# VectorE writes masks into PSUM ahead of the score matmuls, in an attention block followed by six local-attention layers

## The chip, the core and the metric

The kernel runs on one core of a Trainium2 chip. The metric is the device time of one execution in microseconds. Before the change it is 2072.76 us, the median of 3 runs (2070.76 to 2073.34).

The core has five engines that run their own instruction streams in order: TensorE (PE in the profile, with its weight loads listed apart as PEld), VectorE (DVE), ScalarE (ACT), GpSimd (POOL) and SyncE (SP), which here only issues DMAs. PE writes its results into PSUM; the other tiles lie in SBUF.

## The reference, cut to what matters

The input x has 4 sequences of 512 tokens with 128 features. The first stage is a pre-norm causal attention with 16 heads of 64. The future isn't masked out: -50 is added to its scores. The second stage is a pre-norm stack of 6 layers, each a local attention and a GEGLU feed-forward network, with residuals around them.

```python
x = x + attn(layernorm(x), Wq, Wk, Wv, Wr)
    # scores = q k^T / 8 + (-50) * triu(ones, 1); softmax; times v; @ Wr
x = x + ffn(layernorm(x), ...)
    # for each of 6 layers:
    #   t = attn_layer(shift_tokens(x)) + x
    #   x = ffn_layer(shift_tokens(t)) + t
def local_attention(q, k, v):          # windows of 32 tokens
    bk2, bv2 = (look(bk), look(bv))    # a window and the one before it
    mask = (it < jb) | (it > jb + w) | (jb == -1)
    sim = einsum('bhwie,bhwje->bhwij', bq, bk2) * QK_SCALE
    sim = where(mask, -finfo.max, sim)
    out = einsum('bhwij,bhwje->bhwie', softmax(sim, -1), bv2)
```

In a layer q and k are scaled to unit norm per head, multiplied by learned scales and rotated by position. The feed-forward part is a layer norm, a product with W1, a gate by GELU and a product with W2.

## The kernel before

Everything on the engines is issued in an order written out by hand. All matmuls have fp32 operands, but for the two masks, which are bf16.

**First stage** (lines 296 to 495). The work is cut into `Rows`: one sequence b, one pair of heads c (of 8) and one block t of 128 query rows (of 4). The loop runs over 64 slots m; slot m works on two `Rows`, t = 0 and 1 in an even slot, t = 2 and 3 in an odd one. Within a slot:

- `times_v1` (L384) multiplies probabilities of a pair of heads some slots back by v into `o1`, half of the products in each of two slots. After the second half VectorE copies the result to SBUF (L403) at once.
- `scores` (L302) takes a buffer `sc` of two PSUM banks, one per head, and issues four matmuls: for each half of the 512 keys, one for each of the two heads. The two heads' operands lie in different halves of the partitions. There are two `sc` buffers, so a row block takes the buffer of the block two before it, which must have been read by its exponentials.
- `penalty` (L317) adds -50 above the diagonal with two more matmuls per block: identity times a 128x128 triangle `pen`, accumulated into the diagonal block's columns. Both blocks' scores are issued first, then both penalties.
- VectorE takes the negated maximum over the keys (`maximum`, L335); ScalarE takes the exponentials (L348), in two parts with a bias lower by 50 for the keys beyond the diagonal block, and their sums; VectorE adds and inverts the sums (`inverse`, L358 and L359); GpSimd multiplies (`normalise`, L362).
- The probabilities of the slot before are transposed on PE (L373) and copied back by ScalarE (L377) and VectorE (L381). A projection of q, k or v for later slots (L271, L277, L287) lies between.

**The layers** (lines 498 to 1102). A `Unit` is one layer i, one sequence b, one block T of 128 tokens: 96 units in order. `slot(n, ...)` works on four of them at once: it finishes the output of unit n-1, does the attention of unit n, transposes q and k of unit n+1, and projects unit n+2 (`new`). A feed-forward network of a sequence is spread over later slots by three tables: its token shift (`move`), its norm (`norm`: mean, variance and scale in three slots), and its GEGLU steps (`geglu`: three chunks of hidden columns and the output product in four slots). From n = 7 to n = 94 every slot has a GEGLU step, at its end.

The order in `slot` that matters here: `scores(u)` on PE, the projection of Q for `new` with ScalarE's squares, the exponentials, norm steps, the output projection of unit n-1, the rotation of Q (two VectorE products, L570 and L576, and a sum on GpSimd, L587), the transposes of the probabilities (L661, copied by ScalarE, L664) with the projection of K between them, `times_v` (L737, with VectorE's reciprocal and product L746 and L747), the rotation of K, `transpose_o` (L753, VectorE), the sums of squares of Q and of K (`sum_squares`, L565, VectorE), the transposes of q and k, the projection of V, the guard of the norms (L590), the GEGLU step, and the inverse norms (L598 to L606).

`scores` (L684) starts with eight matmuls of a 32x32 identity with a band mask of 64 columns, repeated for 8 pairs of heads (L690). They start the accumulation of every place in two PSUM banks. The 64 products of q and k follow (L700). Then VectorE takes the maximum (L710) and subtracts it (L712), and ScalarE takes the exponential (L718).

PSUM for the layers is three tiles of two banks that rotate (`two_t`, by `part[0] = -n % 3`) and two single banks. In slot n tile 1 of the rotation takes Q's projection, tile 2 K's, tile 0 V's. Tile 2 of slot n is tile 0 of slot n+1, the one that `scores` uses.

Weights: `do_project` loads part j of the next layer's Wqkv right after the last unit of a layer has been projected with it (`load_part`, L501, 512 KB each, on SP's queue). SP also issues the two shifted copies of v in each slot (`shift_v`, L650), the output weights and the feed-forward weights, in program order; a DMA that must wait for an engine holds up those behind it.

## Time and profile before

| | |
|---|---|
| runs, median (lowest to highest) | 2072.76 us (2070.76 to 2073.34) |
| the profiled execution | 2072.4 us, span 2070.6 us |
| PE busy, by matmuls | 2028.4 us (98%), 34382 records |
| VectorE busy | 1640.8 us (79%) |
| ScalarE busy | 1368.2 us (66%) |
| GpSimd busy | 1316.5 us (64%) |

An fp32 matmul shows as two records on PE and two weight loads. The ends of matmuls are modelled, so the distance between starts says more than a duration. By stage, from the trace's busy times in windows: from 52 to 530 us (first stage) PE is busy 475.25 us, VectorE 329.27, ScalarE 308.69, GpSimd 246.42; from 680 to 1990 us (layers) PE 1301.86, VectorE 1114.82, ScalarE 918.19, GpSimd 920.37.

These are groups of the page: line, engine, operation, output and inputs with their shapes, count, then busy time and mean duration, then the engine's idle time before them and what ended most of it.

```profile
L335 DVE TENSOR_REDUCE nm<-ps_sc 128x2 f32<-128x1024 f32 x128 | 155.9, 1218 | 62.9 <-PE ps_sc L323 62.8
L746 DVE RECIPROCAL rden<-ps_att 128x8 f32<-128x8 f32 x192 | 38.8, 202 | 176.8 <-PE ps_att L737 176.7
L565 DVE TENSOR_REDUCE ss<-sq 128x16 f32<-128x1024 f32 x192 | 221.1, 1190 | 0.0
```

The first line is the maximum in the first stage: 128 of them, 1218 ns each, and VectorE idled 62.9 us before them, nearly all of it until the penalty matmuls were done. The second is the reciprocal in the layers, before which VectorE idles 176.8 us in total for `times_v`. The third is the sums of squares, before which it never idles.

### The profile page before, as it was taken

The numbers are of one execution on the slowest core, as the hardware profiler recorded it, in microseconds if no ns is written. First come the engines' busy times: TensorE is split into PE (matmuls) and PEld (weight loads), VectorE is DVE, ScalarE is ACT, GpSimd is POOL, SyncE is SP. The second block draws the span as 40 slices with busy tenths as digits, with TensorE's granted clock in tenths as the row PEclk, the third lists the DMA queues.
The fourth block names the chain that finished last, engine by engine and source line by source line (L and its number), as shares of the span: only waits on it lengthen the run. The fifth ranks groups of instructions, "written<-read, shape, count | busy, mean of one in ns | idle before, by whom it ended". The sixth has DMA issues, their size and how long they took to land.

```text
span 2070.6 us, 77263 instructions
## 1 busy us (share of the span) xinstructions
PE 2028.4 (98%) x34382; PEld 1329.1 (64%) x34382; DVE 1640.8 (79%) x2240; ACT 1368.2 (66%) x2678; POOL 1316.5 (64%) x1432
## 2 busy tenths in 40 slices
PE   7999999999999999999999999999999999999998
PEld 5665555655466666666666666666666666666665
DVE  3766766767698888888888888888888888888885
ACT  3665665666455766676776676776667776677763
POOL 1554554555677677667767667667677767667762
PEclk8999999999999999999999999999999999999999
DMA  3000000000011121111211112111121111211110
GB/s 127 1 1 1 1 1 1 1 1 1 12 44 36 42 67 44 44 44 33 77 44 34 54 36 64 53 35 44 46 64 44 38 51 46 67 41 44 38 45 27
DMA packets 34968, 77.44 MB, mean 37 GB/s; under 512 B 4686, under 2 KB 18764, under 8 KB 34636
## 3 DMA queue, kind: packets, MB, share of 16 engines
q1 hardware_dynamic: 33932, 70.79, 11.8%
q8 instruction: 272, 4.46, 0.9%
q10 hardware_dynamic: 704, 1.70, 0.2%
q14 instruction: 60, 0.49, 0.1%
HBM read 23.50 MB, written 1.05 MB: 12 GB/s over the span
## 4 chain that ended last, share of the span: by engine, by line
PE 91%; DVE 5%; ACT 2%; POOL 1%; issue 1%; DMA 0%; SPq 0%; POOLq 0%; ACTq 0%
PE ps_proj L548 23%; PE ps_one L661 12%; PE ps_one L762 7%; PE ps_att L737 7%; PE ps_sc L308 6%; PE ps_o L393 6%; PE ps_att L700 5%; PE ps_pt L373 5%; PE ps_proj L812 3%; PE ps_proj L813 3%; PE ps_proj L832 3%; PE ps_pj L287 1%; PE ps_att L690 1%; PE ps_pj L277 1%; PE ps_pj L271 1%; PE ps_pj L407 1%
## 5 line engine op out<-in xcount | busy, mean ns | idle before, releaser
L587 POOL TENSOR_TENSOR rot<-rot,t 128x1024 f32<-128x1024 f32 x192 | 454.2, 2366 | 232.6 <-DVE t L576 220.1
L548 PE MATMUL ps_proj<-wqkv,xs 128*128 128x512 f32 x1152 | 569.0, 602 | 0.5 <-PE ps_one L661 0.2
L362 POOL TENSOR_TENSOR pr<-pr,den 128x1024 f32<-128x1024 f32 x128 | 241.0, 1893 | 248.3 <-DVE den L359 238.5
L606 POOL TENSOR_TENSOR rot<-rot,ss 128x1024 f32<-128x1024 f32 x192 | 361.3, 1903 | 7.4
L560 ACT ACTIVATE sq<-ps_proj 128x1024 f32<-128x1024 f32 x192 | 196.4, 1023 | 93.8 <-PE ps_proj L548 93.6
L548 PEld LDWEIGHTS ps_proj<-wqkv,xs 128*128 128x128 f32 x1152 | 188.2, 190 | 102.0 <-issue 92.1
L570 DVE TENSOR_TENSOR rot<-ps_proj,lt 128x1024 f32<-128x1024 f32 x192 | 233.3, 1215 | 10.2 <-ACT sq L560 10.0
L576 DVE TENSOR_TENSOR t<-ps_proj,lt 128x1024 f32<-128x1024 f32 x192 | 232.9, 1213 | 0.0
L348 ACT ACTIVATE pr<-ps_sc,nm 128x128 f32<-128x128 f32 (+3 forms) x448 | 220.3, 509 | 11.8 <-DVE nm L335 8.6
L565 DVE TENSOR_REDUCE ss<-sq 128x16 f32<-128x1024 f32 x192 | 221.1, 1190 | 0.0
L661 PEld LDWEIGHTS ps_one<-ident,rot 128*128 128x128 f32 x1536 | 172.7, 141 | 61.2 <-issue 51.2
L661 PE MATMUL ps_one<-ident,rot 128*128 128x128 f32 x1536 | 205.1, 276 | 1.1 <-POOL xs L170 0.6
L335 DVE TENSOR_REDUCE nm<-ps_sc 128x2 f32<-128x1024 f32 x128 | 155.9, 1218 | 62.9 <-PE ps_sc L323 62.8
L664 ACT COPY pT<-ps_one 128x512 f32<-128x512 f32 x192 | 110.0, 587 | 136.6 <-PE ps_one L661 136.6
L762 PEld LDWEIGHTS ps_one<-aT,wo 128*128 128x128 f32 x1536 | 182.9, 192 | 23.6 <-issue 17.7
L762 PE MATMUL ps_one<-aT,wo 128*128 128x128 f32 x1536 | 189.1, 276 | 0.3 <-ACT tmp_t L852 0.2
L746 DVE RECIPROCAL rden<-ps_att 128x8 f32<-128x8 f32 x192 | 38.8, 202 | 176.8 <-PE ps_att L737 176.7
L648 ACT COPY vt<-ps_proj 128x512 f32<-128x512 f32 x192 | 103.1, 590 | 96.4 <-PE ps_proj L548 96.4
L373 PEld LDWEIGHTS ps_pt<-ident,pr 128*128 128x128 f32 x1024 | 117.4, 142 | 58.5 <-issue 47.4
L664 ACT COPY qT<-ps_one 128x512 f32<-128x512 f32 x192 | 103.1, 589 | 66.1 <-PE ps_one L661 66.1
L377 ACT COPY pT<-ps_pt 128x512 f32<-128x512 f32 x128 | 75.6, 591 | 98.0 <-PE ps_pt L373 98.0
L373 PE MATMUL ps_pt<-ident,pr 128*128 128x128 f32 x1024 | 135.9, 274 | 3.0 <-DVE pT L381 2.4
(178 smaller groups left out, 3763.2 us busy)
## 6 DMA issues: line engine op xcount, KB each, us to landing
vs<-vt SPq DMA_DIRECT2D x96, 390.0 KB, 3.7
vs<-vt SPq DMA_DIRECT2D x72, 130.0 KB, 3.6
wqkv<-in_wqkv_dram SPq DMA_DIRECT2D x18, 512.0 KB, 4.0
vs<-in_zeros_dram SPq DMA_DIRECT2D x24, 130.0 KB, 3.7
wo<-in_wo_dram SPq DMA_DIRECT2D x6, 512.0 KB, 4.2
w<-in_w_dram SPq DMA_DIRECT2D x6, 341.0 KB, 5.9
xr<-in_x_dram SPq DMA_DIRECT2D x3, 256.0 KB, 7.6
scales<-in_scales_dram SPq DMA_DIRECT2D x6, 128.0 KB, 3.1
```

The lines of the kernel that those rows point to most:

```text
L348: nc.scalar.activation(self.pr[:, h, cols], self.sc[:, h, cols], AF.Exp, bias=self.nm[:, part_, h : h + 1], accum_out=self.den[:, part_, h ...
L362: nc.gpsimd.tensor_tensor(self.pr, self.pr, self.den[:, 0].unsqueeze(2).to_broadcast([P, 2, S]), ALU.mult)
L373: nc.tensor.transpose(pt[:, k * P : (k + 1) * P], self.pr[:, h, k * P : (k + 1) * P], ident)
L548: mm(p[:, c, :], lhsT=u.xs[:, u.T * P : (u.T + 1) * P], rhs=wpart[j][:, c * 512 : (c + 1) * 512], start=True, stop=True,)
L565: nc.vector.tensor_reduce(u.ss[:, j * HEADS : (j + 1) * HEADS], heads(u.sq[j]), AX.X, ALU.add)
L570: nc.vector.tensor_tensor(heads(t0), heads(pf), lt[:, u.T, 2 * j].unsqueeze(1).to_broadcast([P, HEADS, HD]), ALU.mult)
L576: nc.vector.tensor_tensor(t1.rearrange("p (h t d) -> p h t d", t=2, d=half), pf.rearrange("p (h t d) -> p h t d", t=2, d=half)[:, :, ::-1, :],
L587: nc.gpsimd.tensor_tensor(u.r[j], u.r[j], u.t1, ALU.add)
L606: nc.gpsimd.tensor_tensor(heads(u.r[j]), heads(u.r[j]), u.ss[:, j * HEADS : (j + 1) * HEADS].unsqueeze(2).to_broadcast([P, HEADS, HD]), AL ...
L661: nc.tensor.transpose(tp[:, c * P : (c + 1) * P], src[:, (4 * g + c) * P : (4 * g + c + 1) * P], ident)
L664: nc.scalar.copy(dst[:, 4 * g : 4 * g + 4, col0 : col0 + P], tp.rearrange("p (c t) -> p c t", c=4))
L762: mm(y[:, 0:P], lhsT=wo_w[0][:, k, :], rhs=u.aT[:, g].rearrange("p (j f) -> p j f", f=P)[:, :, f0 : f0 + W], start=(k == 0), stop=(k == NC ...
```

## The change

- First stage: from slot 4 on the penalty matmuls go. In the slot before, VectorE copies the triangle, now also in fp32 (`pen32`, 64 KB, loaded on SP's queue behind `pen`), into the diagonal block's columns of both heads in the next `sc` buffer (`preset`), ahead of `inverse`, for either row block. The score matmuls add to it.
- `scores` goes over the keys in three pieces instead of two, in every slot: the diagonal block (128 columns), the other half of the keys (256), and the neighbour of the diagonal block (128). So it issues six matmuls per block instead of four.
- The copy of `o1` to SBUF is issued behind the first block's maximum instead of ahead of it.
- Layers: in a slot with a GEGLU step VectorE copies the mask of the next unit, now an fp32 constant (`mask`, 128 KB, loaded on SP's queue ahead of the tables), into tile 2 of the rotation, 1024 columns, after the rotation of K. The next slot's `scores` then issues no band matmuls.
- In slots with n >= 0 the sum of squares of Q moves from behind `transpose_o` to ahead of `times_v`.
- The load of Q's part of the next layer's Wqkv moves from behind Q's projection on SP's queue to behind the transposes of the probabilities on ScalarE's queue.

```diff
+            def preset(self):
+                sc = self.sc = ps1.tile([P, 2, S], F32, tag="sc", name="ps_sc", bufs=2)
+                nc.vector.tensor_copy(
+                    sc[:, :, self.t * P : (self.t + 1) * P], pen32.unsqueeze(1).to_broadcast([P, 2, P])
+                )
             def scores(self):
...
-                for k0 in range(0, S, S // 2):
+                sc, far = self.sc, (1 - t // 2) * 2
+                for k, (k0, n) in enumerate(((t, 1), (far, 2), (t ^ 1, 1))):
+                    cols = slice(k0 * P, (k0 + n) * P)
                     for h in range(2):
                         rows = slice(h * HD, (h + 1) * HD)
                         mm(
-                            sc[:, h, k0 : k0 + S // 2],
+                            sc[:, h, cols],
                             lhsT=qs[b, c][rows, t * P : (t + 1) * P],
-                            rhs=ks[b, c][rows, k0 : k0 + S // 2],
-                            start=(k0 == 0),
-                            stop=False,
+                            rhs=ks[b, c][rows, cols],
+                            start=(k == own),
+                            stop=own or k == 2,
...
             for r in now:
-                r.penalty()
+                if r.late:
+                    r.penalty()
...
             if now:
                 now[0].maximum()
+            if m >= 4:
+                keep()
...
             if now:
+                if 3 <= m < last - 1:
+                    rows[2 * m + 2].preset()
                 now[0].inverse()
                 now[0].normalise()
...
+                if 3 <= m < last - 1:
+                    rows[2 * m + 3].preset()
                 now[1].inverse()
...
+    def preset(u):
+        u.sc = two_t(2, "ps_att")
+        nc.vector.tensor_copy(
+            u.sc.rearrange("p a (c n) -> p a c n", n=2 * W),
+            mask[:, min(u.T, 1)].unsqueeze(2).to_broadcast([P, 2, NC, 2 * W]),
+        )
     def scores(u):
-        sc = two_t(0, "ps_att")
-        for j, h, x_, p0 in PLACES:
+        sc = two_t(0, "ps_att") if u.sc is None else u.sc
+        for j, h, x_, p0 in PLACES if u.sc is None else ():
...
+    def next_part(u, j):
+        if u.b + 1 == B and u.T + 1 == NT and u.i + 1 < L:
+            wpart[j] = load_part(u.i + 1, j, nc.sync if j else nc.scalar)
...
             transpose_p(u, 1)
+        if new:
+            next_part(new, 0)
...
+        if new and n >= 0:
+            sum_squares(new, 0)
         if u:
             times_v(u, 0)
             times_v(u, 1)
...
         if new:
             rotate(new, 1)
             add_rotated(new, 1)
+        if new and geglu and n >= 0:
+            preset(nxt)
         if u:
             transpose_o(u)
+        if new and n < 0:
+            sum_squares(new, 0)
         if new:
-            sum_squares(new, 0)
             sum_squares(new, 1)
```

More of the change, by code (lines that the diff above doesn't have):

```diff
@@ L61, in body @@
     band = const.tile([P, 2, 2 * W], BF16, tag="band", name="band")
+    mask = const.tile([P, 2, 2, 2 * W], F32, tag="mask", name="mask")
     ident16 = const.tile([P, P], BF16, tag="ident16", name="ident16")
@@ L195, in body @@
         pen = s1.tile([P, P], BF16, tag="pen", name="pen")
+        pen32 = s1.tile([P, P], F32, tag="pen32", name="pen32")
         xr = [s1.tile([P, NT, EMB], F32, tag="xr", name=f"xr{b}", bufs=2) for b in range(B)]
@@ L205, in body @@
                 nc.sync.dma_start(out=pen, in_=a["pen"])
+                nc.sync.dma_start(out=pen32, in_=a["pen32"])
         for t_, n_ in ((wq, "wq"), (wk, "wk"), (wv, "wv")):
@@ L210, in body @@
         nc.sync.dma_start(out=band, in_=a["band"])
+        nc.sync.dma_start(out=mask, in_=a["mask"])
         nc.sync.dma_start(out=tabs, in_=a["tabs"])
@@ L299, in __init__ @@
             def __init__(self, b, c, t):
-                self.b, self.c, self.t = b, c, t
+                self.b, self.c, self.t, self.sc = b, c, t, None
+            def preset(self):
[3 more added lines that the diff above has]
+                )
             def scores(self):
                 b, c, t = self.b, self.c, self.t
-                sc = self.sc = ps1.tile([P, 2, S], F32, tag="sc", name="ps_sc", bufs=2)
-                for k0 in range(0, S, S // 2):
+                own = self.sc is not None
+                self.late = not own
+                if not own:
+                    self.sc = ps1.tile([P, 2, S], F32, tag="sc", name="ps_sc", bufs=2)
+                sc, far = self.sc, (1 - t // 2) * 2
+                for k, (k0, n) in enumerate(((t, 1), (far, 2), (t ^ 1, 1))):
+                    cols = slice(k0 * P, (k0 + n) * P)
                     for h in range(2):
@@ L402, in times_v1 @@
                 at = aTs[b, c] = s1c.tile([P, S], F32, tag="aT1", name="aT1", bufs=NC + 2)
-                nc.vector.tensor_copy(at, o)
+                return lambda: nc.vector.tensor_copy(at, o)
+            return lambda: None
         def project_out1(b, y):
@@ L427, in body @@
                 g = m // 2 - 2
-                times_v1(g // NC, g % NC, odd)
+                keep = times_v1(g // NC, g % NC, odd)
             for r in now:
@@ L499, in body, with load_part @@
     s2a = ps2a = s2b = s2 = ps_one = kT_first = vts = None
-    def load_part(i, j):
+    def load_part(i, j, eng=nc.sync):
         w = wts.tile([P, INNER], F32, tag=f"wqkv{j}", name=f"wqkv{j}_{i}")
-        nc.sync.dma_start(out=w, in_=a["wqkv"][i, :, j * INNER : (j + 1) * INNER])
+        eng.dma_start(out=w, in_=a["wqkv"][i, :, j * INNER : (j + 1) * INNER])
         return w
@@ L541, in __init__ @@
             self.i, self.b, self.T = i, b, T
-            self.r, self.sq = [None, None], [None, None]
+            self.r, self.sq, self.sc = [None, None], [None, None], None
     def project(u, j, c0=0, c1=2):
@@ L884, in do_project @@
         project(u, j, c0, c1)
-        if c1 == 2 and u.b + 1 == B and u.T + 1 == NT and u.i + 1 < L:
-            wpart[j] = load_part(u.i + 1, j)
+        if j and c1 == 2:
+            next_part(u, j)
+    def next_part(u, j):
+        if u.b + 1 == B and u.T + 1 == NT and u.i + 1 < L:
+            wpart[j] = load_part(u.i + 1, j, nc.sync if j else nc.scalar)
     def first_slot():
@@ L899, in first_slot @@
         square(new, 0)
-        times_v1(B - 1, NC - 2, 1)
+        times_v1(B - 1, NC - 2, 1)()
         rotate(new, 0)
@@ L911, in first_slot @@
         inverse_norms(new)
-        times_v1(B - 1, NC - 1, 1)
+        times_v1(B - 1, NC - 1, 1)()
         second_step()
@@ L1141, in _constants @@
         band[r : r + W, 1] = np.where(seen, 0.0, NEG)
+    mask = np.repeat(band[:, 1:2, None, :], 2, 2).repeat(2, 1)
+    for r in range(0, P, HD):
+        mask[r + W : r + HD] = mask[r : r + W]
+        mask[r : r + W, 0, 0] = band[r : r + W, 0]
     band = band.astype(ml_dtypes.bfloat16)
@@ L1146, in _constants @@
     zeros = np.zeros((W, 2, NC, HD + 1), f)
-    return {"tabs": tabs, "band": band, "pen": pen, "ident16": ident16, "zeros": zeros}
+    return {"tabs": tabs, "band": band, "mask": mask, "pen": pen, "pen32": pen.astype(f), "ident16": ident16, "zeros": zeros}
 def kernel(**inputs):
```

## The prediction, made before the changed kernel was run

> **What bounds the kernel now.** I read the page first: the busy line and the chain that ended last.

> ```profile
> span 2070.6 us, 77263 instructions
> ...
> PE 91%; DVE 5%; ACT 2%; POOL 1%; issue 1%; DMA 0%; SPq 0%; POOLq 0%; ACTq 0%
> ```

> TensorE's matmuls are 91% of that chain, so an instruction taken from PE counts fully unless another engine is late soon after. The second view is the timeline of two slots of the first stage (start, duration, engine, line, operation, count, in brackets the idle time before and what ended it).

> ```profile
> 421.41 2.00 PE L308 MATMUL ps_sc<-k,q 64*128 64x256 f32 x16
> 423.34 0.40 PE L323 MATMUL ps_sc<-pen,ident 128*128 128x128 bf16 x4
> 423.57 1.04 PE L373 MATMUL ps_pt<-ident,pr 128*128 128x128 f32 x8
> 423.66 1.23 DVE L335 TENSOR_REDUCE nm<-ps_sc 128x2 f32<-128x1024 f32 x1 [2.17 <-PE ps_sc L323]
> ...
> 428.19 2.00 PE L308 MATMUL ps_sc<-k,q 64*128 64x256 f32 x16
> 428.29 0.48 ACT L348 ACTIVATE pr<-ps_sc,nm 128x256 f32<-128x256 f32 x1
> 428.96 0.49 DVE L358 TENSOR_TENSOR den<-den 128x2 f32<-128x2 f32 x1 [1.00 <-ACT pr L348]
> ```

> PE starts one thing as the last stream ends: scores take 1.93 us (421.41 to 423.34), the penalty 0.23 (423.34 to 423.57). VectorE waits 2.17 us for both rows' scores and the penalty. The third view is the timeline of the layers, per engine: PE, VectorE, PE's weight loads, ScalarE.

> ```profile
> 1176.80 1.02 PE L813 MATMUL ps_proj<-hT,w 128*128 128x512 f32 x2
> 1177.75 0.41 PE L690 MATMUL ps_att<-band,ident 64*32 64x512 bf16 x8
> 1177.98 1.46 PE L700 MATMUL ps_att<-kT_first,qT 64*32 64x64 f32 x128
> ...
> 1183.83 1.04 PE L661 MATMUL ps_one<-ident,pr 128*128 128x128 f32 x8
> ```

> ```profile
> 1171.87 0.21 DVE L746 RECIPROCAL rden<-ps_att 128x8 f32<-128x8 f32 x1 [2.02 <-PE ps_att L737]
> ...
> 1174.69 1.22 DVE L576 TENSOR_TENSOR t<-ps_proj,lt 128x1024 f32<-128x1024 f32 x1
> 1175.82 1.23 DVE L753 STREAM_TRANSPOSE aT<-on 128x1024 f32<-128x1024 f32 x1
> 1176.98 2.30 DVE L565 TENSOR_REDUCE ss<-sq 128x16 f32<-128x1024 f32 x2
> 1179.35 0.75 DVE L820 SCALAR_TENSOR_TENSOR tmp_t<-ps_proj,vecs,tmp_t 128x512 f32<-128x512 f32 x1
> ```

> ```profile
> 1183.64 1.00 PEld L661 LDWEIGHTS ps_one<-ident,pr 128*128 128x128 f32 x8 [0.47 <-ACT pr L718]
> ```

> ```profile
> 1182.52 1.06 ACT L718 ACTIVATE pr<-pr 128x1024 f32<-128x1024 f32 x1
> ```

> The band's matmuls hold PE for 0.23 us (1177.75 to 1177.98; eight run side by side). VectorE is nearly full but stands idle about 2 us before L746 in each slot. The weight load of the probabilities' transpose is released by the exponential only 0.19 us before its matmul starts: little is to be gained there beyond that.

> **The change part by part.** *Penalty, first stage.* Slots 4 to 63 lose four penalty matmuls: 60 x 0.23 = 13.8 us off PE.

> *Scores in three pieces.* All 64 slots now issue 12 matmuls in place of 8, with the same columns. The nearest row for a 128-column record is L373: 8 in 0.88 us (423.57 to the next start, 424.45), 0.110 each, against 0.43 / 4 = 0.1075 for a quarter of a 512-column record (L813, 0.86 for two). Eight records more at 0.0025 is 0.02; I take 0.03 a slot, +1.9 us. Bounds: nothing, and a 128-column pair of heads as dear as a 256-column one (1.93 / 4 = 0.48, two pairs more, +0.97 a slot, +62 us). I stay at the low end because loads aren't the limit in the trace: L700 loads 128 weights of 32 columns in about 1.4 us of its slot, 0.011 us each, so 24 loads of 128 columns would need 24 x 4 x 0.011 = 1.1 us, under 1.93.

> [...]

> *Presets, first stage.* Two VectorE copies of 128x256 from SBUF into PSUM a slot. No row has this form. Copies out of PSUM: 128x512 takes 0.680 (L279); operations of 1024 elements take 1.21 (L576). That is 1.04 us per 1000 elements, so 0.68 - 0.27 = 0.41 us. Bounds: 0.28 (the 128x128 operation L776) and 0.68. VectorE is 329 busy in the 478 us from 52 to 530, 69%; 0.82 of some 7.5 us more leaves it under 80%. The first row's preset waits for the same exponential as the inverse behind it; the POOL product behind that starts 0.4 us later (0.8 for the second row), where PE wants its result 0.8 us or more later (POOL ends at 424.44, its transposes start at 425.31). The second row's is the tight one: its buffer is read by the exponential until 428.77, and the next scores of that row start at 428.19 + 0.97 = 429.16. 0.41 us just fits, and the maximum, no longer behind the penalty and the other row (0.97 + 0.23 = 1.2 us earlier), brings the exponentials forward; PE's transposes and the copies between let through perhaps 0.3. I cost it at nothing; with the cover gone it is 60 x 0.41 = 25 us. The o copy behind the maximum is wanted by PE only a slot later.

> *Mask, layers.* Slots 8 to 94 lose the eight band matmuls: at most 87 x 0.23 = 20.0 us. Less where the exponential is already late: after a first GEGLU chunk (22 slots) the 0.19 us bounds it, and I take 0.10; after the second (22) the exponential ends at 1198.27 and its transpose starts at 1198.52, so 0.18 in 17 slots and nothing in the 5 that already idle 0.82 us there; after the third and after the FFN's end (22 + 21) all 0.23. Sum 2.2 + 3.1 + 9.9 = 15.2 us. Floor: 87 x 0.10 = 8.7.

> *Its preset* writes 1024 elements, 1.21 us by L576 and 1.23 by L753 (bounds 0.68, if copies go at the rate of L279 for half as many, and 2.4 for twice L576). It takes the place of one 1.15 us reduction, which moves into the idle 1.6 to 2 us before L746. So L753 starts 1.2 us later (used a slot later), and the second reduction ends 0.06 us later: GpSimd's guard and the GEGLU gate, which waits for ScalarE anyway, hardly notice. PE needs the preset by 1177.75; it would end at 1177.0. Cost nothing; beyond 0.7 us of delay each 0.1 costs 87 x 0.1 = 9 us.

> *The reduction moved* also in slots without a GEGLU step: four PE waits for the exponential there (0.96, 0.54, 0.51, 0.25, at 596 to 667) should shrink; I take -1.5, bounds 0 and -2.3.

> *DMAs.* The penalty's second copy goes out on SP's queue ahead of the second x, one issue (1.73 to 2.21 for pen), and PE waits 3.96 us for that x: +0.5 (0 to 1). The mask's 128 KB delays only tables needed much later. Q's next weights, five loads, go from SP to ScalarE's queue behind the copies of the probabilities; one issue takes 0.5 there, and the square behind it waits 0.22 to 0.28 for PE in any case and is wanted over 3 us later. In the slot of 1254.43 the load would start near 1264 and land 4.0 us later; the next projection of Q starts at 1256.05 + 15.6 = 1271.6. Free; late by all of it, 5 x 4 = 20 us. SP keeps K's load and the two v shifts, wanted a slot later.

> *Sum:* -13.8 + 1.9 - 15.2 - 1.5 + 0.5 = -28.1. The profiled execution took 2072.4 us (span 2070.6 and 1.8 around it), beside a median of 2072.76: **2044.3 us**. Its own range: all gains and no costs, 2072.4 - 13.8 - 20.0 - 2.3 = 2036.3; only 0.15 a slot in the first stage and the floor in the layers, 2072.4 - 9.0 - 8.7 + 0.5 = 2055.

> **Rivals.** *A: the second preset is a new wait on PE.* For it: L308's weight loads already wait on ScalarE's exponential (33.7 us, 43 times). Then the first stage loses 0.41 - 0.20 a slot: 2072.4 + 12.6 - 15.2 - 1.5 + 0.5 = 2068.8. Against it: the 1.2 us that the maximum gains.

> *B, slower: short matmuls bound by their loads.* Place: the three-piece scores. At the upper bound, 2072.4 + 62 - 13.8 - 15.2 - 1.5 + 0.5 = 2104. It decides from 30 / 64 = 0.47 us a slot, a 128-column pair at 0.22 + 0.12 = 0.34 us. For it: L308's loads last 187 ns each, and no row has 64-row weights of 128 columns with so short a stream. Against it: L373 and L700.

> *C, slower: presets held up by GpSimd.*

> ```profile
> 578.12 1.52 DVE L78 TENSOR_SCALAR yt<-rs 128x4 int32<-128x4 int32 x1
> 579.67 1.83 DVE L79 TENSOR_SCALAR y<-yt 128x4 int32<-128x4 int32 x1
> ```

> These take 0.17 us elsewhere; here POOL's product L606 runs beside them (577.71, 3.76 us). A second row's preset so held to the end of L362 (422.55 or 429.44) comes 0.7 us late: 60 x (0.7 - 0.2) = +30, so 2072.4 + 30 - 15.2 - 1.5 + 0.5 = 2086, and more if the mask's is held too. Against it: VectorE's operations with PSUM on one side (L279, 673 to 692 ns) never stretch. [...] No run here shows a write into PSUM.

> *D: nothing*, because the exponentials take back what PE gains: 2072. Against it: PE is busy 475.25 of the 478 us from 52 to 530 and 1301.86 of the 1310 from 680 to 1990, so little waits now.

> **How the numbers follow.** Forecast 0.70, A 0.12, B 0.08, C 0.06, D 0.04. A measurement of this kernel can't tell 0.2% (4.1 us) from no change. Faster: the forecast and half of A with partly hidden waits, 0.77; the same: the other half of A, D and edges, 0.09; slower: B and C, 0.14. Range 2035 to 2070: it takes in the forecast's own 2036 to 2055 and A; above it are B, C and D, 0.18.

> **What would show it.** Right: no penalty matmuls in slots 4 to 63, no band matmuls in slots 8 to 94, scores near 1.96 us from start to start, transposes straight behind them; L335's wait under 1.2 us; presets near 0.41 and 1.21 us; the wait before the reciprocal under 0.9. Wrong: scores over 2.4 us (B), presets with durations that spread (C), PE idle before a row's second scores behind VectorE (A), or PE idle before the probabilities' transposes that grows by what the band took (D).

## The result, and the profile after

The changed kernel takes 2090.9 us (median of 4 runs, 2088.6 to 2097.6), the kernel before 2072.7 (4 runs beside them, 2070.8 to 2073.3). The ratio is 1.010, with a 95% interval from 1.0089 to 1.0112: slower by some 18 us, where 2044 were forecast. The profiled execution took 2088.6 us.

The page of the changed kernel: the span, the chain of waits and the queue that carries PE's instructions.

```profile
span 2086.8 us, 76696 instructions
...
q8 instruction: 269, 4.41, 0.9%
...
PE 91%; DVE 3%; ACT 3%; issue 2%; POOL 1%; DMA 0%; SPq 0%; ACTq 0%; POOLq 0%
```

The chain looks better than before in one place (VectorE 3% for 5%) and worse in another: "issue", time in which PE waited for nothing that the profile shows, has 2% in place of 1%. The page counts 269 packets of instructions, 4.41 MB, each of 16,384 bytes in the trace; the trace has 68,878 PE records, 256 for each packet. The view of waits, PE's own (waited for: us in all, times, longest), says where that time lies, first after, then before:

```profile
PE ps_att L734 <- issue: 32.8, 26, 2.0
PE ps_att L771 <- issue: 3.6, 4, 1.4
...
PE ps_one L686 <- issue: 2.4, 3, 1.3
```

```profile
PE ps_att L700 <- issue: 3.5, 5, 1.4
```

L734 is the old L700, the burst of 128 short matmuls for the scores. With its weight loads it is 256 instructions in about 1.4 us. All issue waits of PE together are 38.8 us after and 4.5 before. Here is the same slot in both kernels, in the timeline (start, duration, engine, line, operation, count, idle time before and its cause); after:

```profile
1191.16 1.23 DVE L713 COPY ps_att<-mask 128x1024 f32<-128x1024 f32 x1
...
1191.46 1.09 ACT L689 COPY kT<-ps_one 128x512 f32<-128x512 f32 x2
...
1192.98 1.19 PEld L734 LDWEIGHTS ps_att<-kT,qT 64*32 64x32 f32 x113 [0.76 <-ACT kT L689]
1192.99 1.35 PE L734 MATMUL ps_att<-kT,qT 64*32 64x64 f32 x113
...
1196.19 0.34 PE L734 MATMUL ps_att<-kT,qT 64*32 64x64 f32 x15 [1.85 <-issue]
```

Before:

```profile
1190.92 1.09 ACT L664 COPY kT<-ps_one 128x512 f32<-128x512 f32 x2
...
1192.44 0.11 PEld L690 LDWEIGHTS <-ident 64*32 64x32 bf16 x8 [0.76 <-issue]
1192.44 0.41 PE L690 MATMUL ps_att<-band,ident 64*32 64x512 bf16 x8
1192.47 1.50 PEld L700 LDWEIGHTS ps_att<-kT,qT 64*32 64x32 f32 x128
1192.67 1.46 PE L700 MATMUL ps_att<-kT,qT 64*32 64x64 f32 x128
```

The preset is done at 1192.39, 0.6 us before the burst, and the burst starts on time. But it stops after 113 records for 1.85 us. In both kernels a block of 256 instructions ends within this burst, some 30 instructions before its end after the change, 54 before it. Counted in the order of the trace, the record behind each such wait is number 194 or 195 of its 256, after as before. The view of DMAs of 7 us in 40 slices shows the packet that carries the next block; the windows begin 3 us before the first QK matmul. After, then before:

```profile
GB/s 428 238 214 71 0 0 0 0 0 0 0 0 0 0 0 0 0 0 0 0 94 0 0 0 0 0 0 0 0 0 0 0 0 0 0 0 0 0 0 0
```

```profile
GB/s 214 167 71 94 0 0 0 0 0 0 0 0 0 0 0 0 0 0 0 0 0 0 0 0 0 0 0 94 0 0 0 0 0 0 0 0 0 0 0 0
```

A slice of 0.175 us at 94 GB/s is 16 KB, one block. After, it starts 0.6 us into the burst (slice 21, 1193.6); before, 2.4 us ahead of it (slice 4, 1190.3). In the 18 waits of over 0.9 us at L734, by the trace's DMA records, PE went on 2.3 to 2.7 us after the packet began. A burst that needs a new block 1.35 us after its start can't have it in time if the packet starts within it.

The starts of the slots' bursts tell what is lost where (us):

| stretch | before | after | difference | forecast |
|---|---|---|---|---|
| first scores to those of slot 4 (start 23.47 and 23.85) | 35.29 | 37.11 | +1.8 | 0 |
| slot 4 to slot 63 of the first stage | 464.42 | 461.28 | -3.1 | -11.9 |
| odd slots, mean | 8.383 | 8.448 | +0.065 | -0.20 |
| even slots, mean | 7.378 | 7.209 | -0.169 | -0.20 |
| layers, slots 0 to 8 | 118.2 | 111.7 | -6.5 | -1.5 |
| layers, slots 8 to 95 | 1357.6 | 1380.3 | +22.7 | -15.2 |

So there are three misses. The large one is the layers'. The second is that the first stage's odd slots gain nothing. The third, at the start, has nothing to do with the change, as the runs below show.

### The profile page after: what moved, and what is told of

It reads as the page before. It is cut to its first block, busy times and chain, and to the rows that moved or that the text cites. A ratio compares the mean times of both kernels' runs of the same rounds, so it can differ in the third digit from the quotient of the medians.

```text
span 2086.8 us, 76696 instructions
## 1 busy us (share of the span) xinstructions
PE 2014.6 (97%) x33958; PEld 1328.0 (64%) x33958; DVE 1791.1 (86%) x2447; ACT 1365.3 (65%) x2678; POOL 1317.0 (63%) x1432
## 3 DMA queue, kind: packets, MB, share of 16 engines
q8 instruction: 269, 4.41, 0.9%
## 4 chain that ended last, share of the span: by engine, by line
PE 91%; DVE 3%; ACT 3%; issue 2%; POOL 1%; DMA 0%; SPq 0%; ACTq 0%; POOLq 0%
PE ps_proj L573 24%; PE ps_one L686 13%; PE ps_one L796 8%; PE ps_att L771 7%; PE ps_att L734 7%; PE ps_sc L325 6%; PE ps_o L410 5%; PE ps_pt L390 4%; PE ps_proj L846 3%; PE ps_proj L847 3%; PE ps_proj L866 3%; PE ps_pj L291 2%; ACT pr L365 1%; PE ps_pj L281 1%; PE ps_pj L425 1%
## 5 line engine op out<-in xcount | busy, mean ns | idle before, releaser
L379 POOL TENSOR_TENSOR pr<-pr,den 128x1024 f32<-128x1024 f32 x128 | 240.9, 1893 | 251.0 <-DVE den L376 250.5
L585 ACT ACTIVATE sq<-ps_proj 128x1024 f32<-128x1024 f32 x192 | 196.5, 1024 | 104.6 <-PE ps_proj L573 101.6
L590 DVE TENSOR_REDUCE ss<-sq 128x16 f32<-128x1024 f32 x192 | 228.9, 1192 | 0.0
L325 PEld LDWEIGHTS ps_sc<-k,q 64*128 64x128 f32 x1536 | 115.4, 189 | 67.9 <-DVE den L376 30.0
L734 PEld LDWEIGHTS ps_att<-kT,qT 64*32 64x32 f32 x9216 | 98.5, 105 | 87.9 <-issue 53.3
L734 PE MATMUL ps_att<-kT,qT 64*32 64x64 f32 x9216 | 113.5, 226 | 32.9 <-issue 32.8
```

Of the source, the lines that this page charges most:

```text
L325: mm(sc[:, h, cols], lhsT=qs[b, c][rows, t * P : (t + 1) * P], rhs=ks[b, c][rows, cols], start=(k == own), stop=own or k == 2, skip_group_ ...
L379: nc.gpsimd.tensor_tensor(self.pr, self.pr, self.den[:, 0].unsqueeze(2).to_broadcast([P, 2, S]), ALU.mult)
L590: nc.vector.tensor_reduce(u.ss[:, j * HEADS : (j + 1) * HEADS], heads(u.sq[j]), AX.X, ALU.add)
L734: mm(sc[p0 : p0 + W, x_, c * 2 * W : (c + 1) * 2 * W], lhsT=u.qT[h * HD : (h + 1) * HD, c, j * W : (j + 1) * W], rhs=u.kT[h * HD : (h + 1) ...
```

## The experiments

**Where PE's blocks end.** Three runs add nothing but instructions: one-column bf16 matmuls into a tile that the real projection then overwrites, once, ahead of the layers.

```diff
 def project(u, j, c0=0, c1=2):
     u.p[j] = p
+    for _ in range(32 if u.n == 0 and j == 0 else 0):
+        mm(p[:, 0, 0:1], lhsT=ident16, rhs=ident16[:, 0:1], start=True, stop=True)
```

32 of them on the changed kernel, 32 on the kernel before, and 128 on the changed kernel. The 0.056 us for each in the expectations is an estimate; the nearest row of before is L323's 256 loads of 128 bf16 columns, 14.4 us in all.

> The changed kernel with 32 one-column bf16 matmuls put once ahead of the layers' first projection: 64 more TensorE instructions, so that every later multiple of 256 falls 64 instructions earlier in the layers' work. Theory (TensorE waits for its next 256 instructions in the last part of the scores' burst): the 26 waits of L734 on issue, 32.8 us, all but vanish; the 32 matmuls cost 32 x 0.056 = 1.8 us; 2088.6 - 33 + 1.8 = 2057 (2050 to 2065). Rival (the presets or VectorE's new order hold TensorE up, wherever its instructions lie): 2088.6 + 1.8 = 2090, the waits stay.

> The kernel before with the same 32 matmuls. Theory: it had few such waits (5, 3.5 us) and four of its slots are 10.24 blocks long, so a shift only deals the few anew: 2072.4 + 1.8 = 2074 (2071 to 2077). Rival (the shift helps for a reason that has nothing to do with the change): it falls by some 30 us here too, to 2042.

> The changed kernel with 128 of the one-column matmuls, 256 instructions: one whole block, so that block ends fall in the layers' work where they fell in the changed kernel. Theory: the waits of L734's burst come back as if nothing had been added, about 26 of them and 33 us, and the 128 matmuls cost 128 x 0.056 = 7.2 us: 2090.9 + 7 = 2098 (2090 to 2104). Rival (any delay or any extra matmuls there help, by their time or by what they do to another engine): near the run with 32 of them, 2060.4 + 96 x 0.056 = 2066.

| run | median us | ratio to before | issue waits in the burst | all issue waits |
|---|---|---|---|---|
| changed + 64 instructions | 2060.4 | 0.9951 (0.9936 to 0.9966) | 5.3 us, 4 | 11.6 |
| before + 64 | 2071.3 | 1.0005 (0.9996 to 1.0015) | 1.4 us, 2 | 3.5 |
| changed + 256 | 2099.4 | 1.0131 (1.0116 to 1.0146) | 33.2 us, 25 | 42.4 |

64 instructions that do nothing take 30 us off the changed kernel. 256 of them, one whole block, bring the waits back to the same burst as if nothing had been added:

```profile
PE ps_att L736 <- issue: 33.2, 25, 2.1
```

The rivals (the presets or VectorE hold PE up; any delay helps) can't give that. The loss is a matter of where block ends fall in the work. In the changed kernel four slots of the layers are 2562 or 2563 PE records, ten blocks of 256 and two or three more, so a block end that falls badly does so in the same kind of slot nearly all through the layers; before, four slots were 2622 or 2623, and block ends wandered.

**The parts alone.** The first stage's part without the layers', and the layers' part without the first stage's.

> Only the first stage's part (scores in three pieces, presets, the later copy of o, the second copy of the penalty); the layers and the loads as before. Theory: the first stage gains nothing net, since the odd slots' second preset ends too late and the full clock comes back 1.8 us later at the start; the layers' slots are as long in instructions as before: 2072.4 - 0.6 = 2072 (2067 to 2077). Rival (the first stage's gain is there as forecast, all of the loss is the layers'): 2072.4 - 13.8 + 1.9 + 0.5 = 2061.

> Only the layers' part (mask preset, no band matmuls, the reduction and Q's load moved); the first stage as before. Slots are 640 TensorE instructions long, as in the changed kernel, but the layers start 32 instructions later in their block, so that block ends fall 32 instructions earlier. Theory: without block waits 2072.4 - 20 = 2052; with them as often as in the changed kernel 2087; waits are expected only where a block still ends in the burst's last 60 instructions, about a third of the places, so 2064 (2052 to 2076). Rival (the preset itself costs the time): 2087, with waits on VectorE ahead of L734.

The first stage alone: 2070.7 us, ratio 0.9997 (0.9987 to 1.0006). It is worth 2.9 us between slots 4 and 63 (461.5), as in the whole change, not 11.9. The layers alone: 2075.3 us, ratio 1.0015 (1.0003 to 1.0026). That is above what I had laid down as likely, though inside the range; the trace has 18.3 us of issue waits, 12.6 in the burst (11 times). I had guessed where the bad places begin, and too narrowly.

**The odd slots of the first stage.** The timeline of an odd slot of the changed kernel, and the start of the even one behind it:

```profile
408.96 0.58 ACT L394 COPY pT<-ps_pt 128x512 f32<-128x512 f32 x1 [2.35 <-PE ps_pt L390]
...
412.89 2.24 PE L325 MATMUL ps_sc<-k,q 64*128 64x128 f32 x24
413.25 0.21 ACT L365 ACTIVATION_READ_ACCUMULATOR pr<-ps_sc,nm 128x1 f32 x1
413.50 0.43 DVE L310 COPY ps_sc<-pen 128x256 f32<-128x256 f32 x1 [0.70 <-ACT pr L365]
...
420.61 0.42 DVE L310 COPY ps_sc<-pen 128x256 f32<-128x256 f32 x1
420.66 2.03 PE L325 MATMUL ps_sc<-k,q 64*128 64x128 f32 x24
```

In the odd slot the second row's preset ends at 413.93, and its matmuls would start at 412.89 + 0.98 = 413.87. PE's 24 records take 2.24 us; in the even slot, whose preset ends 0.37 us after the start of the slot's scores, where this one ends 1.04 us after it, they take 2.03. The run to test it keeps the second row's two penalty matmuls in odd slots:

```diff
-    if 3 <= m < last - 1:
+    if 3 <= m < last - 1 and odd:
         rows[2 * m + 3].preset()
```

> The changed kernel, but the second row of the first stage's odd slots keeps its two penalty matmuls and gets no preset. Theory for the first stage (the preset after four exponentials ends 0.1 us too late, and TensorE loses 0.2 us with it): the odd slots' mean falls from 8.456 us (8.383 in the kernel before) to 8.383 + 0.03 - 0.115 = 8.30; rival (the odd slots lose time to something else): 8.456 + 0.115 = 8.57. For the layers: 30 x 4 = 120 instructions more ahead of them, which puts the block ends of every second slot into the last part of the scores' burst, of both kinds: 2 x 21 waits of some 1.6 us in place of 26: 2090.9 - 5 - 35 + 67 = 2118 (2095 to 2125), slower by it although the first stage is shorter. Rival (block ends do not matter): 2090.9 - 5 = 2086.

The odd slots' mean fell to 8.315 (8.30 expected, 8.57 by the rival). As two of the penalty matmuls came back (0.115 us), the late preset cost 8.45 - 8.315 + 0.115 = 0.25 us a slot. In the changed kernel's trace the second row starts late in 22 of the 29 odd slots, by 0.10 to 0.44 us and by 0.16 on average over all 29; the rest of the 0.25 was not taken apart. The kernel as a whole took 2142.9 us, above the range I gave, ratio 1.035 (1.031 to 1.038), with 42 waits in the burst:

```profile
PE ps_att L734 <- issue: 71.4, 42, 3.2
```

So 120 instructions in the first stage, which made that stage 4 us shorter, cost 52 us in the layers. The count of waits was as expected, each a little longer (1.7 us). All issue waits are 76.2 us for 38.8, which is 37 of the 52. The mean granted clock also fell, from 0.995 in the changed kernel to 0.985 here: behind the start the trace has 43.7 us at half the clock, for 6.5.

**What hides the mask's preset.** The run with 64 instructions more, with the first reduction back behind the transpose of o. PE's instructions and their order are the same.

```diff
-        if new and n >= 0:
-            sum_squares(new, 0)
         if u:
             times_v(u, 0)
...
         if new:
+            sum_squares(new, 0)
             sum_squares(new, 1)
```

> The run with 64 instructions more, with the first reduction put back behind the transpose of o, as in the kernel before; TensorE's instructions and their order are the same. Theory (the moved reduction made room for the mask's preset and brought forward the inverse norms in the slots without a GEGLU step): slots 0 to 8 take 3.5 us longer, and in slots 8 to 94 the second reduction, its guard and the gate behind it come 1.2 us later: at least 2060.4 + 3.5 = 2064, and as much as 0.3 a slot more, 2090, if the gate then ends last before the next scores. Rival (the place of the reduction is of no account): 2060.4, within 3.

2136.9 us, ratio 1.0313 (1.0296 to 1.0331), 76 us above its partner, more than I had allowed. Slots 0 to 8 take 118.7 us, for 114.7 in the partner and 118.2 in the kernel before, so most of what these slots gain comes from the moved reduction. The timeline of a later slot shows the rest:

```profile
1102.03 1.48 PE L736 MATMUL ps_att<-kT,qT 64*32 64x64 f32 x128
1102.41 2.30 DVE L592 TENSOR_REDUCE ss<-sq 128x16 f32<-128x1024 f32 x2
1104.63 0.74 DVE L856 SCALAR_TENSOR_TENSOR tmp_t<-ps_proj,vecs,tmp_t 85x512 f32<-85x512 f32 x1
1105.29 1.21 DVE L746 TENSOR_REDUCE mx<-ps_att 128x16 f32<-128x1024 f32 x1
```

The burst ends at 1103.5, but VectorE is 1.8 us late with the maximum, since preset, transpose, two reductions and the gate stand in a row. Then the exponential is late, and with it PE:

```profile
PE ps_one L688 <- ACT pr L754: 66.5, 86, 1.2
```

**Q's next weights.** The run with 64 instructions more, with Q's load on SP's queue behind the projection, as before.

> The run with 64 instructions more, with Q's next weights loaded as in the kernel before (on SP's queue, behind the projection). The prediction costed the later load at nothing: 2060.4, within 3. Rival (the later load is late for the first projection of the next layer, five times 4 us): 2040; or it spared a transfer next to v's shift: 2065 and more.

2061.5 us (2059.0 to 2062.7) beside 2060.4 (2059.1 to 2061.8): no difference.

**Why the band's eight matmuls counted.** In the kernel before, block ends fell just as badly now and then (the slot shown above), and still there was hardly a wait. What stood between the FFN chunk's matmuls and the burst was the band: 16 instructions with loads that need no kT. After the change the profile puts the wait of the burst's first load down to ScalarE's copy of kT, in 44 of the 96 bursts and in 21 more to that of kT_first; before, it puts the wait of the band's load to nothing. PE's weight loads, after and before:

```profile
PEld ps_att L734 <- ACT kT L689: 34.1, 44, 0.8
```

```profile
PEld L690 <- issue: 73.0, 96, 0.8
```

Two runs put eight matmuls back that add zeros to one column each, once ahead of the burst, once behind it. The count per slot is the same, 656 instructions.

```diff
+    def zeros_on(u, sc):
+        for j, h, x_, p0 in PLACES if u.sc is not None else ():
+            rows = slice(h * HD, (h + 1) * HD)
+            o = (1 - h) * HD
+            mm(
+                sc[p0 : p0 + W, x_, 0:1],
+                lhsT=ident16[rows, h * HD : h * HD + W],
+                rhs=ident16[rows, o : o + 1],
...
+        zeros_on(u, sc)
         for c in range(NC):
             for j, h, x_, p0 in PLACES:
```

> The changed kernel with eight one-column bf16 matmuls that add zeros, in the band's old place ahead of the scores' burst (slots 8 to 94): 16 instructions that wait for no copy of kT, and 656 in a slot as in the kernel before, so that block ends wander through the slot. Both forms of the theory (a fixed place of the block ends; the band's 16 instructions let the fetch start earlier) expect few waits, as in the kernel before (some 4 us): 2060.4 - 1.8 - 8 + 87 x 0.08 = 2057 (2050 to 2064). Rival (the loss in the burst comes from the mask's preset): 2090 and more.

> The same eight matmuls behind the burst in place of ahead of it: also 656 instructions in a slot, but nothing between the FFN's chunk and the burst. If only the fixed place of the block ends did it: as the run with them ahead, 2057 (2050 to 2064). If the band's instructions also kept the fetch early: block ends wander through the bad quarter of the burst in the three kinds of slot that follow a chunk, 65 x 65 / 256 = 16 waits of 1.7 us, so 2057 + 28 = 2085 (2070 to 2090).

Ahead: 2053.5 us, ratio 0.9912 (0.9896 to 0.9929), 3.9 us of issue waits in all. Behind: 2101.6 us, above the range I gave, ratio 1.015 (1.012 to 1.018), 47.1 us of issue waits (26 waits in the burst and at the zeros, where I expected 16). A fixed place of the block ends is thus not all of it: behind the burst the same instructions let the block ends wander, and it is worse.

A count of PE's records settles how much the place alone does. Take the bursts of slots 8 to 94 in which a block ends within the last 64 of the 256 instructions, and how many of them have a wait of PE there:

| kernel | block ends in the last 64 | with a wait |
|---|---|---|
| before | 20 | 1 |
| changed | 40 | 23 |
| zeros ahead | 21 | 0 |
| zeros behind | 21 | 17 |

With the band or the zeros ahead, the packet of the next block had begun 1.2 to 3.0 us before the burst's first load in every one of these bursts but the one that waited. In the 40 bursts with a wait of the other two kernels it began between 0.8 us before that load and 1.2 us after it. The band did not cover everything: the other four waits of the kernel before lie in slots 1, 3, 5 and 7, ahead of which no GEGLU step stands.

With the zeros ahead, the timeline is that of the kernel before, at 0.04 us in place of 0.23 (the 0.08 of the expectation was an estimate):

```profile
1178.97 0.11 PEld L722 LDWEIGHTS <-ident 64*32 64x32 bf16 x8 [0.76 <-issue]
1178.97 0.20 PE L722 MATMUL ps_att<-ident 64*32 64x1 bf16 x8
1179.00 1.32 PEld L748 LDWEIGHTS ps_att<-kT,qT 64*32 64x32 f32 x128
1179.01 1.47 PE L748 MATMUL ps_att<-kT,qT 64*32 64x64 f32 x128
```

What remains open is the inside of it: by which rule the next block is asked for, and whether it is put off by a load that waits for kT or only by there being nothing to issue ahead of the burst. In 4 of the 23 bursts with a wait the first load's own wait isn't put down to kT, and no run looks into PE's queue.

**Versions that beat both.** First by place: twelve of the odd slots keep the penalty matmuls, and one one-column matmul is added, 50 instructions in all.

> The changed kernel, but in the twelve odd slots with the longest waits the second row keeps its penalty matmuls, and one one-column matmul is added: 50 instructions more ahead of the layers, where the run with 64 had its remaining 11 us of issue waits as block ends reached the front of a burst late in the layers. Theory: 2060.4 - 31 x 0.056 (the other one-column matmuls) - 12 x 0.27 (tight slots) - 8 (three quarters of those waits) = 2047 (2042 to 2054), faster than both kernels. Rival (what is left of the loss is VectorE's): 2060 or above.

2055.3 us, ratio 0.9915 (0.9900 to 0.9930), 8.5 us of issue waits; faster than both kernels, but just outside what I expected, since the waits did not shrink to a quarter. Then by cause: the zeros ahead of the burst, and the penalty matmuls in all odd slots.

> The eight zero-adding matmuls ahead of the burst, and the penalty matmuls kept for the second row of the first stage's odd slots: the two mends together. Theory: the odd slots' mean is 8.315 as in the run with the penalty alone (8.451 without), 29 x 0.136 = 3.9 us; the 120 instructions more that cost some 50 us there cost nothing here, since the weight loads ahead of the burst no longer wait: 2053.5 - 4 = 2049.5 (2045 to 2056). Rival (the 120 instructions put the block ends in a bad place here too): 2070 and more.

2048.4 us (2047.0 to 2049.1), ratio 0.9883 (0.9866 to 0.9899): 24 us under the kernel before. The odd slots' mean is 8.316, and the 120 instructions that cost 52 us without the zeros cost nothing with them (3.8 us of issue waits).

**The start.** In the changed kernel's profile the first scores run at half the clock. The same line there, and in the run with the first stage's part alone, which has the same instructions up to there:

```profile
23.85 3.79 PE L325 MATMUL ps_sc<-k,q 64*128 64x128 f32 x24 [0.88 <-DVE k L283]
```

```profile
24.06 2.03 PE L325 MATMUL ps_sc<-k,q 64*128 64x128 f32 x24 [0.88 <-DVE k L283]
```

The full clock was granted at 27.5 us in the one and at 23.0 in the other, and between 19.5 and 29.1 over all fourteen profiles, early and late for the same code (22.4 in the run with 64 instructions more, 29.1 in its partner with the reduction put back). In the eight profiles that have it by 23.1 us the stretch from the first scores to slot 4 takes 35.3 to 35.4 us, in the six that get it from 27.5 us on 37.0 to 37.7. The 1.8 us of the table are that execution's.

## Why the prediction was wrong, point by point

**The mask in the layers (-15.2).** The step that failed. It priced the eight band matmuls as 0.23 us of PE's time, and the prediction's first reading, that an instruction taken from PE "counts fully unless another engine is late soon after", left out PE's own supply of instructions. As work they were worth what was said: with the zeros ahead, slots 8 to 95 take 1344.7 us, 12.9 less than before, or 16.4 without the zeros' 87 x 0.04. But they also stood ahead of the burst as instructions that need no kT, and without them the next block comes too late: 38.8 us of issue waits for 4.5, +34 us. The wait was in the profile of before, small (3.5 us, 5 times at L700), beside a queue named "instruction"; it is in no term and no rival.

**The presets in the first stage (nothing).** The size was right (0.42 us for 0.41, 410 to 429 ns, no spread), and for the second row the prediction found that it "just fits", although its own figures end it at 428.77 + 0.41 = 429.18, 0.02 us past the 429.16 it has to meet. What failed is that the maximum's 1.2 us would bring the exponentials forward. ScalarE has the copy of the transposed probabilities ahead of them in its queue, and waits 2.35 us for PE's transposes there, as the first line of the first stage's fence shows. So the second row's exponentials end 0.6 us after the next scores' start, as before. Rival A's wait is there in the odd slots and not in the even ones, and smaller than it had it (+0.065 us a slot, where A had +0.21): the stretch gained 3.1 us in place of 11.9.

**Scores in three pieces (+1.9).** Right: 420.66 to 422.61 is 1.95 us, and Rival B is dead. The 24 loads last 189 ns each on average (L325) and would take 4.5 us one after another, by an estimate of 24 x 0.189; they fit in 1.95 here. The two heads' loads lie in different rows, but no run shows whether that is why.

**The mask's preset (1.21 us, at nothing).** Right, with the reason given: 1.23 us, and it is hidden only because the reduction moved. The price without that cover was put at 0.5 us beyond the free 0.7, 45 us; it is 76 less some 4 in slots 0 to 8.

**The moved reduction (-1.5, at most -2.3).** Too small: slots 0 to 8 gain 6.5 us, and 6.2 with the zeros ahead. Issue waits there are 1.3 us less, so 5.2 of the 6.5 are something else. The four waits of PE for the exponential that the prediction counted, 2.3 us, are all gone after the change. So is one that it didn't count: 1.8 us at 582.88, put down to VectorE's transposed x (`xT`, L776), which is back, at 2.4 us, where the reduction is put back.

**Q's load (nothing) and the penalty's second copy (+0.5).** The first is right by its run. The first scores started 0.4 us later in the profile. Over all profiles they start at 23.67 to 24.18 in the eleven with the second copy and at 20.96 to 23.47 in the three without, so the +0.5 is not contradicted; three starts don't give its size.

**Rival C.** The presets never stretch beside GpSimd: the 67 of 120 that run beside one of its instructions take 415 to 429 ns. Another VectorE operation does stretch: the bias (L356, SBUF to SBUF, 128x2), which now runs beside GpSimd's product, takes 364 ns on average for 195 before, up to 1.58 us; the 43 that take over 0.2 us all run beside L379, GpSimd's product. This may be part of the odd slots' loss. In the ten odd slots with 0.93 us for it in the slot ahead, ScalarE then waits 0.16 us for the second row's maximum, and the second row's scores start 0.11 us late. No run tests that by itself.

**The sum.** 2044.3, with +8.8 for the first stage, +1.7 for the start (2.2 for the 0.5 allowed), +34.3 for the blocks and -3.7 for the reduction (5.2 beside the issue waits, for 1.5), is 2085.4; the profiled execution took 2088.6. Of the rest, 2.3 lies in slots 8 to 95, where 22.7 less the 35.6 of issue waits in these slots leaves a gain of 12.9 for the 15.2 forecast, and 1.0 between the two stages and behind the last burst.

## What to carry to other kernels

Where PE runs hundreds of tiny matmuls in a burst, count its instructions as well as its time: a block of 256 is gone in 1.4 us here, and its successor takes 2.3 us and more to come. An "issue" wait that falls at the same count modulo 256 (record 194 or 195 here) is the sign, and adding a whole block and a part of one, once, ahead of the work is a cheap test. Before cheap instructions ahead of such a burst are removed, see whether they are the only ones there that don't wait for the burst's own operands; a stand-in of 0.04 us kept the cover here. And when an engine's work is freed earlier, look for what its successor's queue holds ahead of it before counting the time as won.
